# Seven products for eight in the second projection of a gated layer, on three of four blocks of tokens

## Chip, cores and metric

One core of one Trainium2 chip. The metric is the device time of one execution in microseconds; before and after are compared as medians of several executions. Engine names follow the profile: PE is TensorE's matmul stream and PEld its weight loads, DVE is VectorE, ACT is ScalarE, POOL is GpSimd, SP is the engine that issues most transfers.

## The reference

A transformer block in float32 on `x` of 2 x 1024 tokens and 256 features: self attention (16 heads of 64), cross attention to 154 context tokens, and a gated layer. All matmuls run in float32. What matters here is the last of the three:

```python
h = _layernorm(x, ln3_g, ln3_b)
p = h @ ff_w1 + ff_b1                 # 256 -> 2 x 1024
a, gate = (p[..., :D_FF], p[..., D_FF:])
h = a * jax.nn.gelu(gate, approximate=False) @ ff_w2 + ff_b2   # 1024 -> 256
return h + x
```

The second projection is the product of `a * gelu(gate)` (2048 tokens x 1024) with `ff_w2` (1024 x 256), added to the residual `x`.

## The kernel before

The whole kernel is recorded under a manual schedule: the order in which Python calls the helpers is the order in which each engine meets its instructions. Every engine has one queue and takes its instructions in that order. There are no due times or costs; the tile framework only adds the waits.

The attention stages fill the first 900 us. The gated layer then treats the 2048 tokens as NPR = 4 blocks ("pairs" in the code) of 512 tokens. A block is split into two token halves j of BT = 256 tokens. The 1024 inner features are NF = 8 chunks f of 128. A gate n = 8 * block + f (0 to 31) computes chunk f for the block's 512 tokens, by a seven-product scheme of its own (`product`, L1029): seven 128x128 by 128x256 products into three PSUM tiles `pa`, `pb`, `pc`. It is spread over two steps k of the main loop:

- Even k, `gate_first(n)`: product 1, then `gate_last(n - 1)` with product 4 of the gate before, products 6 and 5. So four products on PE.
- Odd k, `gate_second(n)`: products 2, 7, 3. So three products on PE.

The results go through ACT (a copy L1048, two GELUs L1066 and L1072) and DVE (L1052, L1054, L1068, L1071, L1080). POOL then multiplies value and gate into the buffers `ub[block][j][:, f, :]`: L1073 writes half j=1 (called from `gate_second`), L1082 writes half j=0 (called from `gate_last`, so one step later).

When gate f=7 of a block has been issued, the second projection of that block is queued in `sums`: 4 token tiles x 8 chunks = 32 slots, each one matmul (`sum_slot`, L1095) with 128 columns of `ub` as stationary operand and the 256 columns of `w2[:, f, :]` as moving operand. After the eighth chunk of a tile DVE adds the bank to the residual (L1105) and an output transfer is issued (L1106). Each step of the next block takes two slots from the queue, so 32 slots fill its 16 steps. The last block's slots run after the loop:

```python
            for _ in range(min(2, len(sums))):
                run(sum_slot)
            flush(stores)
            run_work(0 if k == 1 else 1 + k % 2, k % 2)
            if later and (k <= len(CG) + 2 or k > 2 * NF):
                later.pop(0)()
        gate_last(FU - 1)
        while sums:
            run(sum_slot)
            flush(stores)
```

POOL has other work in the same loop: the addition of the output bias to the residual (L324, one 128x256 addition in each step from k=17 to 31, popped from `later`) and the token sums of the gates' own scheme (`token_sums`, L1012 to L1015, four additions of 128x256 at k=8, 24 and 40).

PSUM: `sum_tile` and `mm_tile` have two banks each, `part_tile` four. `hold_gated` keeps both weight matrices of the layer in SBUF; `w2[:, f, d]` is chunk f of `ff_w2`.

Of the kernel before, what the change touches and what calls it, by code (L numbers as in the profile page):

```python
# [8 lines left out]
F32 = mybir.dt.float32  # L9
AF = mybir.ActivationFunctionType  # L10
ALU = mybir.AluOpType
AX = mybir.AxisListType

P = 128
# [4 lines left out]
def tile_transformer_block(ctx: ExitStack, tc: tile.TileContext, a: dict, out: bass.AP):  # L19
    nc = tc.nc  # L20
    x, cond = a["x"], a["ctx_768"]
    w = {k[len("L0_xattn_"):]: v for k, v in a.items() if k.startswith("L0_xattn_")}
# [9 lines left out]
    NT = S // P  # L32
    GT = 4
# [14 lines left out]
    QH = S // 2  # L48
    GH = QH // QG
    NK = HB // KB  # L50
    TG = HB // T
    NF = DF // P
    SH = GH // 2
    TF = 2
# [8 lines left out]
    pt_ = ctx.enter_context(tc.tile_pool(name="pt", bufs=2))  # L63
# [9 lines left out]
    def sum_tile(name):  # L73

        return ps_o.tile([P, HB], F32, tag="po", name=name)


    xt = {
        (b, g): const.tile([P, GT, D], F32, tag=f"x{b}{g}", name=f"x{b}{g}")
        for b in range(B) for g in range(NG)  # L80
    }
# [10 lines left out]
    names = ["ln1_g", "ln1_b", "ln2_g", "ln2_b", "ln3_g", "ln3_b", "ff_b1"]  # L92
# [5 lines left out]
    for n in names:  # L98
        k = n_of[n]
# [8 lines left out]
    for n in names[:2]:  # L108
        for r0 in range(0, P, HR):
            (nc.scalar if n == names[0] else nc.sync).dma_start(  # L110
                out=cols[r0:r0 + HR, row_of[n]:row_of[n] + NH],
                in_=w[n].rearrange("(r p) -> p r", p=HR),
# [54 lines left out]
    for n in names[2:]:  # L167
        own = rows[row_of[n] - n_cols:row_of[n] - n_cols + n_of[n], :]
        p = HR if n in twice else P
# [202 lines left out]
    def take_both(dst, pq, mul=None, t0=0, n=S // 2, shared=False):  # L372

        for r in range(2):
            k0, own = r * S // 2 + t0, pq[r][:, :n]
            if mul is not None:
                if shared and r:
                    nc.vector.tensor_scalar(
                        dst[:, k0:k0 + n], own, mul, 1.0, op0=ALU.mult, op1=ALU.mult)
                else:  # L380
                    nc.scalar.activation(dst[:, k0:k0 + n], own, AF.Copy, scale=mul)  # L381
                continue

            dk = dst.rearrange("p (h n j) -> p n h j", h=2, j=KB)[:, k0 // QG:(k0 + n) // QG]
            own = own.rearrange("p (n h j) -> p n h j", h=2, j=KB)
            if shared and r:
                nc.vector.tensor_copy(dk, own)
            else:
                nc.scalar.copy(dk, own)
# [172 lines left out]
    def run(piece):  # L562
        done = piece()
        if done is not None:
            (adds if getattr(done, "adds", False) else stores).append(done)

    def flush(queue):
        for fn in queue:
            fn()
        queue.clear()  # L570

    def run_work(n, n_side, bank=None, n_sum=0):

        while n > 0 and work:
            n -= work[0].banks
            run(work.pop(0))
        for _ in range(min(n_side, len(side))):  # L580
            needs_bank, needs, fn = side[0]
            if needs_bank and not bank and n <= 0 or not added.issuperset(needs):
                break
            if needs_bank and not bank:
                n -= 1
            spare["bank"] = bank or mm_tile
            run(fn)
            side.pop(0)
        for i in range(min(max(n, 0) + n_sum, len(outs))):
            spare["out"] = mm_tile if i < n else sum_tile  # L590
            run(outs.pop(0))
# [360 lines left out]
    NPR = B * 2  # L952
    BT = S // 4
    FU = NPR * NF
    wsum, wh, ub, psum, pools = {}, {}, {}, {}, {}

    def hold_gated():

        wf = pt_.tile([P, 2 * NK, QH // 2], F32, tag="pT", name="wf").rearrange("p a b -> p (a b)")
        n1, n2 = NC * 2 * DF, NF * D  # L960
        w1 = wf[:, :n1].rearrange("p (c h f) -> p c h f", c=NC, h=2)
        w2 = wf[:, n1:n1 + n2].rearrange("p (f d) -> p f d", f=NF)
        pTc["pairs"] = wf[:, n1 + n2:n1 + n2 + 2 * NM * 2 * NT * KB].rearrange(
            "p (a m j q) -> p a m j q", a=2, m=NM, j=2)

        def part1(c, h, f):
            f0 = h * DF + f
            nc.sync.dma_start(out=w1[:, c, h, f:f + HB], in_=w["ff_w1"][c * P:(c + 1) * P, f0:f0 + HB])

        def part2(f):  # L970
            nc.sync.dma_start(
                out=w2[:, f:f + 2, :],
                in_=w["ff_w2"][f * P:(f + 2) * P, :].rearrange("(f p) d -> p f d", p=P),
            )

        parts = [
            lambda c=c, h=h, f=f: part1(c, h, f)
            for c in range(NC) for h in range(2) for f in range(0, DF, HB)
        ]
        parts.extend(lambda f=f: part2(f) for f in range(0, NF, 2))  # L980
        return w1, w2, parts
# [39 lines left out]
    def product(n, i, into, first):  # L1021

        pair, f = divmod(n, NF)
        own = slice(f * P, (f + 1) * P)
        lhs = {
            1: w1[:, 0, 1, own], 2: w1[:, 1, 1, own], 3: wsum[4][:, own], 4: w1[:, 1, 0, own],
            5: wsum[1][:, own], 6: wsum[2][:, own], 7: w1[:, 0, 0, own],
        }[i]
        nc.tensor.matmul(  # L1029
            into[:, :BT], lhsT=lhs, rhs=wh[pair][i], start=first, stop=True,  # L1030
            skip_group_check=True)
# [24 lines left out]
    def biases(n):  # L1056
        c = row_of["ff_b1"] + n % NF
        return cols[:, c:c + 1], cols[:, c + NF:c + NF + 1]
# [16 lines left out]
    def gate_last(n):  # L1075

        pair, f = divmod(n, NF)
        pa, pb, pc, own = psum.pop(n)
        product(n, 4, pb, False)
        nc.vector.scalar_tensor_tensor(  # L1080
            own[:, 0, :], pb[:, :BT], biases(n)[0], own[:, 0, :], op0=ALU.add, op1=ALU.add)
        nc.gpsimd.tensor_tensor(ub[pair][0][:, f, :], own[:, 0, :], own[:, 3, :], ALU.mult)  # L1082
        if f == NF - 1:
            sums.extend((pair, i, e) for i in range(2 * TF) for e in range(NF))

    sums, summed = [], {}

    def sum_slot():

        pair, i, f = sums.pop(0)  # L1090
        if f == 0:
            summed[pair] = sum_tile(f"pf{pair}_{i}")
        own = summed[pair]
        j, e = divmod(i, TF)
        nc.tensor.matmul(  # L1095
            own[:, :D], lhsT=ub[pair][j][:, f, e * P:(e + 1) * P], rhs=w2[:, f, :],
            start=(f == 0), stop=(f == NF - 1),
        )
        if f < NF - 1:
            return None  # L1100
        b, t = divmod(pair * 2 * TF + i, NT)

        def store():
            xs = xt[b, t // GT][:, t % GT, :]
            nc.vector.tensor_tensor(xs, own[:, :D], xs, ALU.add)  # L1105
            (nc.scalar if pair == NPR - 1 and i % 2 else nc.sync).dma_start(  # L1106
                out=out[b, t * P:(t + 1) * P, :], in_=xs)

        return store


    with tc.manual_schedule():
# [11 lines left out]
        own = [ps_s.tile([P, 2, HB], F32, tag="s", name=f"first_{r}") for r in range(2)]  # L1124
# [7 lines left out]
        def take(what, i):  # L1132
            at = banks[what] if i < 2 else banks["k2"]
            take_both(qk["sa", 0, 0]["qk".index(what)], at, scale if what == "q" else None,
                      i * P, 2 * P, shared=True)
# [36 lines left out]
        for p in range(SA):  # L1172
# [18 lines left out]
            h, hg = divmod(p, SH)  # L1191
            ui, n = divmod(p, 2 * SH)
# [8 lines left out]
            if hg == LAG:  # L1201
                f = (ui - NPAIR // 2 - 1) * EC
# [10 lines left out]
        for c in range(CA):  # L1213
# [7 lines left out]
            if c == SH + 1:  # L1221

                w1, w2, parts = hold_gated()
# [3 lines left out]
            ui, n = divmod(c, len(CG))  # L1227
# [53 lines left out]
            elif n == 2:  # L1281
# [3 lines left out]
                elif ui == HP:  # L1285
                    wo["ca"] = const.tile([P, NPAIR, D], F32, tag="wo", name="ca_wo")
                    later[:0] = [lambda i=i: nc.sync.dma_start(
                        out=wo["ca"][:, i, :], in_=w["ca_wo"][i * P:(i + 1) * P, :])
# [20 lines left out]
        for k in range(2 * FU):  # L1309
            c = CA + k  # L1310
            if k == 0:
                run_work(0, 0, n_sum=2)
            flush(adds)
            (gate_second if k % 2 else gate_first)(k // 2)
            flush(stores)
            flush(lates)
            if k == 2 * len(CG) + 1:
                norm_beside("ff", B - 1)
            cross_drain(c)
            if k % 2:  # L1320
                cross_weigh(c - 1 if k == len(CG) + 2 else c)
            cross_regroup(c)
            if k == len(CG) + 2:
                out_pieces("ca", B - 1, NQ - 1, out_order("ca"))
            if k % (2 * NF) == NF and k < 2 * FU - 2 * NF:
                token_sums(k // (2 * NF) + 1)
            for _ in range(min(2, len(sums))):
                run(sum_slot)
            flush(stores)
            run_work(0 if k == 1 else 1 + k % 2, k % 2)  # L1330
            if later and (k <= len(CG) + 2 or k > 2 * NF):
                later.pop(0)()
        gate_last(FU - 1)
        while sums:
            run(sum_slot)
            flush(stores)


# [31 lines left out]
```

## Time and profile before

| | us |
|---|---|
| median of 3 runs | 1085.54 (1083.54 to 1085.69) |
| the profiled execution | 1084.96 |
| its span, first to last instruction | 1083.2 |
| PE busy in the span | 1067.0 |
| POOL busy | 727.1 |
| DVE busy | 878.7 |
| ACT busy | 643.5 |
| gated loop's gates 8 to 31 (950.60 to 1065.45) | 114.85 |
| second projection of the last block, from 1066.04 | 13.83 |

A line of the profile names the source line, engine, operation, the output and input tiles, and the shape; a PE matmul in float32 appears as two records. "Idle before" is how long the engine stood still ahead of an instruction, with the instruction that released it behind an arrow. PEclk is the clock granted to TensorE, as a share of full speed; it is 1.00 for this execution.

### The profile page before, as it was taken

What the parts mean: (1) busy time and instruction counts of PE and PEld (TensorE: products, weight loads), DVE (VectorE), ACT (ScalarE), POOL (GpSimd) and SP (SyncE); (2) the same over time, 40 slices, a digit from 0 to 9 for tenths busy, and PEclk for the clock granted to TensorE, in tenths of its full rate; (3) what the DMA queues carried; (4) which work ended last, traced back from release to release, by engine and by line L of the source; (5) the groups of instructions that cost most, each with busy time, mean ns of one, the idle gap of its engine ahead of it and who ended that gap; (6) DMA issues with size and microseconds to landing.
All of it is one profiled execution on the core that took longest, in us unless ns stands there. A gap on an engine that the chain in (4) does not pass through costs nothing.

```text
span 1083.2 us, 46388 instructions
## 1 busy us (share of the span) xinstructions
PE 1067.0 (99%) x19156; PEld 703.2 (65%) x19156; DVE 878.7 (81%) x1297; ACT 643.5 (59%) x2062; POOL 727.1 (67%) x1552
## 2 busy tenths in 40 slices
PE   8999999999999999999999999999999999999998
PEld 6556556556565565575665655566776677788887
DVE  5799999998989989999999889968877887654442
ACT  5766666777667657666776776656555554242321
POOL 2677777777777777677777777776756785475321
PEclk9999999999999999999999999999999999999999
DMA  3222122112111121111111101136765545000000
GB/s 91 68 70 52 39 48 53 43 43 50 32 43 34 30 50 38 34 43 34 33 42 25 43 14 38 29 79 150 191 157 125 119 107 118 1 10 15 11 14 30
DMA packets 104724, 60.81 MB, mean 56 GB/s; under 512 B 32378, under 2 KB 95298, under 8 KB 104514
## 3 DMA queue, kind: packets, MB, share of 16 engines
q1 hardware_dynamic: 103138, 57.07, 22.2%
q8 instruction: 151, 2.47, 1.0%
q10 hardware_dynamic: 1376, 0.79, 0.2%
q14 instruction: 59, 0.48, 0.1%
HBM read 27.91 MB, written 2.10 MB: 28 GB/s over the span
## 4 chain that ended last, share of the span: by engine, by line
PE 83%; DVE 4%; POOL 4%; DMA 3%; SPq 2%; ACT 2%; issue 1%; POOLq 0%; DVEq 0%; ACTq 0%
PE po L549 18%; PE s L497 17%; PE py_sa L471 5%; PE pf L1095 5%; PE py_ca L471 5%; PE pk_sa L366 4%; PE pv_sa L397 4%; PE poc L908 4%; PE pq_ca L366 4%; PE pq_sa L366 4%; PE pb L1029 4%; DMA st<-st 3%; PE sc L828 2%; PE pa L1029 2%; PE pc L1029 2%; SPq L518 2%
## 5 line engine op out<-in xcount | busy, mean ns | idle before, releaser
L619 POOL TENSOR_SCALAR p<-p,rd,ee 128x512 f32<-128x512 f32 x512 | 390.4, 768 | 90.8 <-DVE rd L609 87.7
L508 ACT ACTIVATE p<-s,st 128x512 f32<-128x512 f32 x512 | 345.0, 686 | 171.1 <-DVE st L681 163.7
L681 DVE TENSOR_REDUCE st<-s 128x2 f32<-128x1024 f32 x256 | 308.5, 1206 | 56.9 <-issue 19.0
L644 DVE STREAM_TRANSPOSE pT<-p 128x1024 f32<-128x1024 f32 x256 | 302.7, 1219 | 2.4 <-POOL p L619 2.1
L497 PE MATMUL s<-k_sa,q_sa 64*32 64x512 f32 x4096 | 252.8, 591 | 3.3 <-ACT p L508 2.5
L549 PE MATMUL po<-pT,v_sa 64*32 64x256 f32 x8192 | 237.1, 376 | 1.0 <-DVE pT L644 1.0
L549 PEld LDWEIGHTS po<-pT,v_sa 64*32 64x32 f32 x8192 | 172.9, 106 | 76.2 <-issue 31.2
L497 PEld LDWEIGHTS s<-k_sa,q_sa 64*32 64x32 f32 x4096 | 78.4, 106 | 104.6 <-issue 57.6
L845 ACT ACTIVATE p<-sc,neg 128x154 f32<-128x154 f32 x256 | 96.1, 403 | 83.0 <-DVE rden L853 79.3
L856 POOL TENSOR_SCALAR p<-p,rden 128x154 f32<-128x154 f32 x256 | 96.8, 398 | 56.7 <-DVE rden L853 56.5
L508 ACT ACTIVATION_READ_ACCUMULATOR p<-s,st 128x1 f32 x512 | 103.9, 203 | 0.0
L526 POOL TENSOR_TENSOR dd<-st 128x8 f32<-128x8 f32 x128 | 25.6, 200 | 74.9 <-DMA st<-st 73.0
L397 PEld LDWEIGHTS pv_sa<-sa_wv,hT_ln 64*128 64x128 f32 x1024 | 58.5, 188 | 14.2 <-issue 8.4
L397 PE MATMUL pv_sa<-sa_wv,hT_ln 64*128 64x128 f32 x1024 | 61.8, 275 | 0.0
L471 PE MATMUL py_ca<-ca_wo,o_ca 128*128 128x256 f32 x256 | 60.0, 382 | 0.5 <-DVE o_ca L922 0.5
L366 PE MATMUL pq_ca<-hT_ln,ca_wq 64*64 64x512 f32 (+1 forms) x544 | 60.1, 590 | 0.0
L471 PE MATMUL py_sa<-sa_wo,o_sa 128*128 128x256 f32 x256 | 59.7, 385 | 0.2 <-ACT v_sa L406 0.2
L471 PEld LDWEIGHTS py_sa<-sa_wo,o_sa 128*128 128x128 f32 x256 | 47.3, 190 | 18.2 <-issue 6.9
L834 DVE TENSOR_REDUCE neg<-sc 128x6 f32<-128x924 f32 (+1 forms) x48 | 47.9, 998 | 13.7 <-PE sc L828 13.3
L366 PE MATMUL pq_sa<-hT_ln,sa_wq 64*32 64x512 f32 (+1 forms) x976 | 56.6, 586 | 0.0
L366 PE MATMUL pk_sa<-hT_ln,sa_wk 64*32 64x512 f32 x960 | 56.2, 590 | 0.3 <-ACT q_sa L381 0.3
L845 ACT ACTIVATION_READ_ACCUMULATOR p<-sc,neg 128x1 f32 x256 | 56.1, 219 | 0.0
(121 smaller groups left out, 1418.9 us busy)
## 6 DMA issues: line engine op xcount, KB each, us to landing
wf<-pT_ca SPq DMA_DIRECT2D x128, 128.0 KB
st<-st SPq DMA_DIRECT2D x512, 1.0 KB
v_sa<-v_sa SPq DMA_DIRECT2D x32, 256.0 KB
sa_wq<-in_L_xattn_sa_wq_dram SPq DMA_DIRECT2D x32, 128.0 KB
sa_wk<-in_L_xattn_sa_wk_dram SPq DMA_DIRECT2D x32, 128.0 KB
sa_wv<-in_L_xattn_sa_wv_dram SPq DMA_DIRECT2D x32, 128.0 KB
ca_wq<-in_L_xattn_ca_wq_dram SPq DMA_DIRECT2D x32, 128.0 KB
wf<-in_L_xattn_ff_w_dram SPq DMA_DIRECT2D x12, 256.0 KB
```

The source lines that it names most:

```text
L366: nc.tensor.matmul(pq[r][f:f + m, at:at + n], lhsT=wt[own, c, f:f + m], rhs=h[own, c, t0:t0 + n], start=(c == 0), stop=(c == NH - 1), tile ...
L397: nc.tensor.matmul(pv[r][:, i * P:(i + 1) * P], lhsT=h[own, c, i * P:(i + 1) * P], rhs=wt[own, c, :], start=(c == 0), stop=(c == NH - 1), ...
L471: nc.tensor.matmul(py[:, e * D:(e + 1) * D], lhsT=o[:, i, (t + e) * P:(t + e + 1) * P], rhs=wo[kind][:, g * HP + i, :], start=(i == 0), st ...
L497: nc.tensor.matmul(sc[a4 * KB:(a4 + 1) * KB, j, :], lhsT=q[r, c:c + KB], rhs=k[r, h * HB:(h + 1) * HB], start=True, stop=True, tile_positi ...
L508: nc.scalar.activation(pr[:, j, :], sc[:, j, :], AF.Exp, bias=st[:, 0, 0, i, j:j + 1], accum_out=st[:, 0, 1, i, j:j + 1],)
L549: nc.tensor.matmul(po[a2][d:d + KB, :QH // 2], lhsT=v[r, t, e, d:d + KB], rhs=pT[r, d // DH * NK + n, :], start=(t == 0 and e == 0), stop= ...
L619: nc.gpsimd.tensor_scalar(pr[:, j, :], pr[:, j, :], own["rd"][:, c:c + 1], own["ee"][:, 0, c:c + 1], op0=ALU.mult, op1=ALU.mult,)
L644: nc.vector.transpose(halves[h][:, :, c:c + KB], slots[p]["p"][i].rearrange("p j (n k) -> p (j n) k", k=KB))
L681: nc.vector.tensor_reduce(st[:, 0, 0, i, :], sc[i], AX.X, ALU.max, negate=True)
L845: nc.scalar.activation(pr_[:, j, i, :T], sc[:, j, i * T:(i + 1) * T], AF.Exp, bias=neg[:, j, i:i + 1], accum_out=den[:, j, i:i + 1],)
L856: nc.gpsimd.tensor_scalar(pr_[:, j, i, :T], pr_[:, j, i, :T], rden[:, j, i:i + 1], 1.0, op0=ALU.mult, op1=ALU.mult,)
L1029: nc.tensor.matmul(into[:, :BT], lhsT=lhs, rhs=wh[pair][i], start=first, stop=True, skip_group_check=True)
```

## The change

For blocks 1, 2 and 3 (`FAST`) the second projection of each half j is computed as a 2x2 block product. The half's 256 tokens are two groups e of 128 tokens, its 1024 features are two groups of four chunks, and the 256 outputs are two groups of 128. Each of the resulting quarters of tokens A and weights B has four chunks. Seven products of quarters take the place of eight:

- Four sums of weight quarters T1 to T4 (`quick_weights`) are made once, on POOL, at steps k=22 to 25: four operations of 128x512.
- For each chunk c and half j, four sums of token quarters (`quick_tokens`) are made on POOL: S1, S2, S3 (written in place over A21) and S4, four operations of 128x128. They are queued in `combos` when gate f = 4 + c of the block has been issued, and popped four per step for k > 26; the rest follows after the loop.
- A unit g = 0 to 6 (`fast_sum`) is one product of quarters: four matmuls of 128 columns, accumulated over the four chunks. Units share banks: g=1 adds into the bank of g=0, g=3 and g=4 into that of g=2, g=6 into that of g=5. After each unit the bank is added to the residual: after g=0 by an ACT copy and a POOL addition of 128x384 (DVE in the last block), after the others by a DVE addition of 128x128.
- A step takes one unit (or two old slots). Block 0 keeps the 32 slots. Blocks 1 and 2 go half by half, j=0 then j=1; block 3 alternates j=1 and j=0 for each g.
- Output transfers of a half are issued after g=5 and g=6.

A sum made by POOL is read by PE: g=1 reads the gates' products of f=4 to 7, g=2 reads S2, g=3 reads S3, g=5 S1, g=6 S4. The new scratch tile `quick` takes the `pT` buffer that the cross attention leaves.

```diff
--- before.py
+++ after.py
@@ -1080,14 +1080,114 @@
         nc.vector.scalar_tensor_tensor(
             own[:, 0, :], pb[:, :BT], biases(n)[0], own[:, 0, :], op0=ALU.add, op1=ALU.add)
         nc.gpsimd.tensor_tensor(ub[pair][0][:, f, :], own[:, 0, :], own[:, 3, :], ALU.mult)
-        if f == NF - 1:
-            sums.extend((pair, i, e) for i in range(2 * TF) for e in range(NF))
-
-    sums, summed = [], {}
-
-    def sum_slot():
-
-        pair, i, f = sums.pop(0)
+        if pair in FAST and f >= NHF:
+            for j in (1, 0) if pair == NPR - 1 else (0, 1):
+                combos.extend(quick_tokens(pair, j, f - NHF))
+        if f == NF - 1 and pair in FAST:
+            order = [(j, g) for j in range(2) for g in range(7)]
+            if pair == NPR - 1:
+                order = [(j, g) for g in range(7) for j in (1, 0)]
+            sums.extend((lambda j=j, g=g: fast_sum(pair, j, g), 2) for j, g in order)
+        elif f == NF - 1:
+            sums.extend(
+                (lambda i=i, e=e: sum_slot(pair, i, e), 1) for i in range(2 * TF) for e in range(NF))
+
+    sums, summed, quick, combos = [], {}, {}, []
+    FAST = range(1, NPR)
+    NHF = NF // 2
+
+    def hold_quick():
+
+        own = pt_.tile([P, 2 * NK, QH // 2], F32, tag="pT", name="quick").rearrange("p a b -> p (a b)")
+        at = 0
+
+        def take(*dims):
+            nonlocal at
+            n = 1
+            for d in dims:
+                n *= d
+            view = own[:, at:at + n]
+            at += n
+            names = "abc"[:len(dims)]
+            return view.rearrange(
+                f"p ({' '.join(names)}) -> p {' '.join(names)}", **dict(zip(names, dims)))
+
+        for i in (1, 2, 3, 4):
+            quick["w", i] = take(NHF, P)
+        for i in range(3):
+            quick["u", i] = take(3, NHF, P)
+        for i in range(2):
+            quick["own", i] = take(P)
+
+    def quick_weights():
+
+        (b11, b12), (b21, b22) = (
+            [w2[:, h * NHF:(h + 1) * NHF, d * P:(d + 1) * P] for d in range(2)] for h in range(2))
+        t1, t2, t3, t4 = (quick["w", i] for i in (1, 2, 3, 4))
+        tt = nc.gpsimd.tensor_tensor
+        return [
+            lambda: tt(t1, b12, b11, ALU.subtract),
+            lambda: tt(t2, b22, t1, ALU.subtract),
+            lambda: tt(t3, b22, b12, ALU.subtract),
+            lambda: tt(t4, b21, t2, ALU.subtract),
+        ]
+
+    def quick_tokens(pair, j, c):
+
+        u, own = ub[pair][j], quick["u", (2 * pair + j) % 3]
+        (a11, a12), (a21, a22) = (
+            [u[:, h * NHF + c, e * P:(e + 1) * P] for h in range(2)] for e in range(2))
+        s1, s2, s4 = (own[:, i, c, :] for i in range(3))
+        tt = nc.gpsimd.tensor_tensor
+        return [
+            lambda: tt(s1, a21, a22, ALU.add),
+            lambda: tt(s2, s1, a11, ALU.subtract),
+            lambda: tt(a21, a11, a21, ALU.subtract),
+            lambda: tt(s4, a12, s2, ALU.subtract),
+        ]
+
+    def fast_sum(pair, j, g):
+
+        u, own = ub[pair][j], quick["u", (2 * pair + j) % 3]
+        (a11, a12), (a21, a22) = (
+            [u[:, h * NHF:(h + 1) * NHF, e * P:(e + 1) * P] for h in range(2)] for e in range(2))
+        lhs = (a11, a12, own[:, 1], a21, a22, own[:, 0], own[:, 2])[g]
+        rhs = (
+            w2[:, :NHF, :P], w2[:, NHF:, :P], quick["w", 2], quick["w", 3], quick["w", 4],
+            quick["w", 1], w2[:, NHF:, P:])[g]
+        if g in (0, 2, 5):
+            bank = sum_tile
+            if pair == NPR - 1:
+                bank = {0: sum_tile, 2: mm_tile, 5: part_tile}[g]
+            summed[j] = bank(f"pq{pair}_{j}_{g}")
+        into = summed[j][:, :P]
+        for c in range(NHF):
+            nc.tensor.matmul(
+                into, lhsT=lhs[:, c, :], rhs=rhs[:, c, :], start=(g in (0, 2, 5) and c == 0),
+                stop=(c == NHF - 1), skip_group_check=True)
+        b, t = divmod(pair * 2 * TF + 2 * j, NT)
+        xs = xt[b, t // GT][:, t % GT:t % GT + 2, :].rearrange("p t (h d) -> p (t h) d", d=P)
+
+        def store():
+            if g == 0:
+                nc.scalar.copy(quick["own", j], into)
+                (nc.vector if pair == NPR - 1 else nc.gpsimd).tensor_tensor(
+                    xs[:, 1:, :], xs[:, 1:, :],
+                    quick["own", j].unsqueeze(1).to_broadcast([P, 3, P]), ALU.add)
+                return
+            q = (None, 0, 1, 3, 2, 3, 1)[g]
+            nc.vector.tensor_tensor(xs[:, q, :], into, xs[:, q, :], ALU.add)
+            if g > 4:
+                e = 6 - g
+                queue = nc.scalar if pair == NPR - 1 and e else nc.sync
+                queue.dma_start(
+                    out=out[b, (t + e) * P:(t + e + 1) * P, :],
+                    in_=xt[b, (t + e) // GT][:, (t + e) % GT, :])
+
+        return store
+
+    def sum_slot(pair, i, f):
+
         if f == 0:
             summed[pair] = sum_tile(f"pf{pair}_{i}")
         own = summed[pair]
@@ -1324,15 +1424,29 @@
                 out_pieces("ca", B - 1, NQ - 1, out_order("ca"))
             if k % (2 * NF) == NF and k < 2 * FU - 2 * NF:
                 token_sums(k // (2 * NF) + 1)
-            for _ in range(min(2, len(sums))):
-                run(sum_slot)
+            n_left = 2
+            while n_left > 0 and sums:
+                fn, n = sums.pop(0)
+                n_left -= n
+                run(fn)
             flush(stores)
+            if k == 2 * NF + 2:
+                hold_quick()
+            if 2 * NF + 6 <= k < 2 * NF + 10:
+                if not combos:
+                    combos.extend(quick_weights())
+                combos.pop(0)()
+            elif k > 2 * NF + 10:
+                for _ in range(min(4, len(combos))):
+                    combos.pop(0)()
             run_work(0 if k == 1 else 1 + k % 2, k % 2)
             if later and (k <= len(CG) + 2 or k > 2 * NF):
                 later.pop(0)()
         gate_last(FU - 1)
+        while combos:
+            combos.pop(0)()
         while sums:
-            run(sum_slot)
+            run(sums.pop(0)[0])
             flush(stores)
```

## The prediction

> **What bounds the kernel now.** I read the page's busy shares and slices first, then a table of windows over the gated layer, then POOL's timeline where the change puts its additions, then the forms of weight loads and products.
>
> ```profile
> PE 1067.0 (99%) x19156; PEld 703.2 (65%) x19156; DVE 878.7 (81%) x1297; ACT 643.5 (59%) x2062; POOL 727.1 (67%) x1552
> ...
> PE   8999999999999999999999999999999999999998
> ```
>
> TensorE is busy to the end of the span, so removed products are removed time, if nothing else makes PE wait.
>
> ```profile
> 950.60:970.48 19.88, 19.88 (x99) 17.51 (x98) 9.27 (x23) 8.36 (x19) 13.10 (x21) 1.00 0.02 7
> 970.48:989.47 18.99, 18.99 (x89) 16.72 (x88) 9.32 (x22) 5.42 (x13) 13.86 (x20) 1.00 0.05 15
> 989.47:1027.46 37.99, 37.99 (x178) 33.44 (x177) 18.71 (x44) 10.84 (x25) 14.99 (x21) 1.00 0.04 14
> ```
>
> Columns: the window, its length, then busy PE, PEld, DVE, ACT, POOL, and PE's granted clock. The first two windows are block 1 (gates 8 to 11, then 12 to 15; one starts every 4.75 us), the third is block 2. PE never pauses. DVE and ACT have room. POOL is busy 27.0 of block 1's 38.9 us (the gates' products, the output bias, token sums) but only 15.0 of 38.0 in block 2.
>
> ```profile
> 970.86 0.73 POOL L1073 TENSOR_TENSOR u<-own 128x256 f32<-128x256 f32 x1 [1.97 <-ACT own L1072]
> 971.55 0.72 POOL L324 TENSOR_TENSOR x<-x,ff_b 128x256 f32<-128x256 f32 x1
> 972.23 0.73 POOL L1082 TENSOR_TENSOR u<-own 128x256 f32<-128x256 f32 x1
> 972.92 0.72 POOL L1012 TENSOR_TENSOR hs<-hT_ln 128x256 f32<-128x256 f32 x1
> 973.72 0.73 POOL L1013 TENSOR_TENSOR hs<-hT_ln,hs 128x256 f32<-128x256 f32 x1
> ```
>
> Start to start, a two-input 128x256 on POOL costs 0.685 us; one that needs the result just before it starts 0.80 after it, so such a dependence costs 0.11.
>
> ```profile
> L1095 PEld LDWEIGHTS pf<-wf,u 128*128 128x128 f32 x224 | 42.6, 190 | 5.8
> L1095 PE MATMUL pf<-wf,u 128*128 128x256 f32 x224 | 55.0, 379 | 0.0
> ```
>
> ```profile
> 14.74 1.86 PEld L366 LDWEIGHTS first_k<-hT_ln,sa_wk 64*128 64x128 f32 x32 [0.17 <-issue]
> ```
>
> ```profile
> 1066.04 13.83 PE pf L1095 x64
> ```
>
> These are forms of instructions (busy, mean ns), a timeline row of early weight loads, and the last row of the chain of waits. A product is two records. Sixty-four of 256 columns take 13.83 us: 0.216 each, with their 190 ns loads hidden.
>
> **TensorE's saving.** A block's second projection is now 32 products, 64 records, 13.83 us. After: two halves x 7 units x 4 products x 2 records = 112 records of 128 columns, each with a fresh 128-column load. No full-height row shows that. The nearest is the timeline row above: 64-row loads of 128 columns feeding 128 moving columns, two row groups side by side, 32 loads in 1.86 us. Per row group that is (1.86-0.19)/15 = 0.111; single records stand 0.112 apart. Lower bound 0.109 (transposes, L284, 128 columns); upper bound 0.19, the load's whole duration, if nothing overlapped. I take 0.112: the loads there are equally long (188 ns) and follow each other as fast. So 12.54 us, **-1.29 a block, -3.9 for three**. A unit is 8 x 0.112 = 0.90, against 0.86 for two slots before; a block has 14 units for 16 steps, so its last gate has none.
>
> [...]
>
> **What POOL gets.** In the built order, each of gates 4 to 7 of a block brings 8 additions of 128x128, in fours (`quick_tokens`). Price of one: two-input rows span 128x8 (next start after 0.17 to 0.28) to 128x256 (0.685); a straight line gives 0.42. From below, a one-input 128x154 stands 0.37 apart (L856), some 0.33 at 128; from above, 0.685. I take 0.42, since both ends have two inputs. A group of four has one immediate dependence: 4 x 0.42 + 0.11 = 1.79. The four weight sums, 128x512, come to 1.17 each on the same line; `fast_sum`'s 128x384 addition to 0.94.
>
> Per gate of two steps POOL then has in block 1: two products 1.37, two bias additions 1.37, two groups 3.58: 6.3 us, where PE passes in 4.75. The queue is in order, so the gate products that the sums read stand behind all this.
>
> **Block 1 to 2.** I follow POOL from 967.48 (L1082 of gate 10 in the trace). That product, a weight sum and a bias addition end at 970.02; gate 11's L1073 is ready at 970.86 as before. From there POOL never idles. L1073, weight sum, bias, L1082: 974.09. Token sums (2.85 in the trace): 976.94. Weight sum, bias, L1073 of 12, weight sum, bias, L1082, bias: 982.70. Then until L1082 of gate 15 is through: 6 products, 5 bias additions, 5 groups = 11 x 0.685 + 5 x 1.79 = 16.49, so 999.19. PE begins gate 16 at 989.47 (trace), then 1.73 (four products), unit g=0 0.90, three products 1.30: unit g=1 starts at 993.40, and its fourth product, wanting gate 15's result, at 994.07. With 0.1 for the signal (DVE to PE shows 0.06 at 945.06) PE **stops 5.2 us**. PE's later work is queued behind that matmul. Next, g=2 wants S2 of the last chunk: after 999.19 the 0.94, a group, L1073 of 16, then 0.42 + 0.53: 1003.55. PE arrives at 999.51 + 1.73 + 0.67 = 1001.91 and stops another **1.7**. Sum 6.9.
>
> **Block 2 to 3.** No bias additions. POOL takes up L1082 of gate 20 when ready, 1.63 after gate 21 starts. Until L1082 of gate 23 is through: 7 products 4.80, six groups 10.74, three more dependences 0.33, 1.0 of idle for gate 21's L1073: 18.5 after gate 21's start. PE wants it at 2 x 4.82 + 3.03 (gate 23 has no units) + 1.73 + 0.90 + 1.30 + 0.67 = 17.3. **Stop 1.3** with the signal.
>
> **The end.** Blocks' halves alternate, and 12 additions plus gate 31's last product remain on POOL. By the same queue, counted from gate 29's start: L1073 of 31 ends at 15.8, L1082 at 18.3, the two S2 at 19.3 and 21.1. PE finishes gate 31 at 13.45, including 0.35 because its last product follows L1068 without a unit between. It wants these at 15.9, 16.8, 19.3, and 20.3 as stops push it on: **0.35 + 1.6 + 0.05 + 0.9 = 2.9**.
>
> Hidden: fourteen ACT and DVE stores a block instead of four (128x256 takes 0.42 on DVE, 512 columns 0.69, so 128 about 0.29) have at least one gate step, or another unit of 0.90, before their bank is written again; without that cover each would cost about 0.5. At the end the last DVE addition is 0.13 shorter. Output transfers on SP wait behind nothing but each other, since SP has no other issues left in blocks 2 and 3; the last four leave within 3 us on two queues: 0 to 0.3, I take 0.
>
> **Sum:** -3.9 + 6.9 + 1.3 + 2.9 - 0.1 = **+7.1**. The profiled execution took 1084.96 us for a span of 1083.2, so 1092.1; the median of three is 0.6 higher. I say **1092.4 us**.
>
> The clock: the trace shows a start at half rate, the warm-up transposes 0.213 instead of 0.109 apart for 3.26 us, and no drop after stops of up to 1.08 us. A drop after the 5.2 us stop would lose 1.6 us, but PE waits 1.7 there for S2 anyway. I take 0, range 0 to 1.6.
>
> [...]
>
> **Rivals.** *POOL keeps up* (faster). One price decides: the 128x128 addition. At 0.33 (the one-input row) stops fall to about 4.3 and balance the saving; at 0.25 only the 0.35 is left: 1081.5. For it: POOL idles 23 us of block 2. Against: two-input rows cost 2.1 ns an element, and block 1's bias additions. 0.06 for clearly faster, 0.04 for a tie.
>
> *Loads bind* (slower still). At 0.19 a record a block takes 21.3 us, +7.5, and a slower PE leaves POOL 5.6 us of stops: -3.9 becomes +22.4, in all +28: 1113. Against: the 64-row rows. 0.05.
>
> *Forecast*, 0.85: the price from 0.36 (+2.5) to 0.50 (+14), 1087.5 to 1099, plus 1.6 of clock. Range with the tie's edge: 1086.5 to 1099.5. Measurement cannot tell less than about 0.2% (2.2 us) from no change. Faster 0.06, same 0.04, slower 0.90.
>
> **What would show it.** Right: PE idle before L1165 released by POOL, some 5 us near 994 and 2 near 1002, POOL without a gap from 971 to 1005, additions at L1143 to L1146 near 0.45 us long, and L1165 records 0.112 apart. Wrong: PE without gaps at 994, L1143 under 0.33 long, or L1165 0.19 apart.

## The result, and the profile after

The changed kernel takes 1092.19 us in the median (1091.17 to 1095.51), against 1084.54 us for the kernel before on the same chip (1082.49 to 1085.69): a ratio of 1.0080 over all executions, 95% interval 1.0063 to 1.0097 (the ratio of the two medians is 1.0071). It is slower, as forecast. The forecast was 1092.4 us.

The profiled execution of the changed kernel took 1095.51 us for a span of 1093.7 us, 3.3 us above the median. Its gate 16 starts at 991.35, 1.88 us later than in the trace of before, and PE's work ahead of that is the same and without a pause in the gates before. I therefore compare from gate 16 to the end of the span: 102.37 us here, 93.70 before, **+8.67 us**.

First the page's busy shares and slices:

```profile
PE 1070.7 (98%) x19300; PEld 708.1 (65%) x19300; DVE 884.7 (81%) x1323; ACT 645.5 (59%) x2068; POOL 779.9 (71%) x1656
...
PE   8999999999999999999999999999999999998998
```

POOL has 53 us more than before (779.9 for 727.1), and PE is below nine tenths in one more slice, the 37th (984 to 1012 us). The windows over the gated layer of the changed kernel show where (window, its length, busy PE, PEld, DVE, ACT, POOL, granted clock, DMA share, GB/s). The first line is gates 12 to 15, the second block 2, the third block 3's gates 24 to 30, then come four windows of 3.41 us:

```profile
972.36:991.35 18.99, 18.99 (x89) 16.72 (x88) 9.32 (x22) 5.42 (x13) 18.37 (x28) 1.00 0.05 15
991.35:1035.22 43.87, 38.69 (x225) 35.10 (x224) 20.35 (x52) 11.09 (x26) 35.41 (x66) 0.96 0.05 16
1035.22:1070.47 35.25, 34.14 (x212) 31.33 (x211) 18.72 (x49) 10.28 (x24) 24.23 (x46) 1.00 0.04 12
...
997.78:1001.20 3.42, 0.00 (x0) 0.00 (x0) 0.00 (x0) 0.00 (x0) 3.34 (x8) 1.00 0.00 0
1001.20:1004.61 3.41, 3.33 (x9) 2.79 (x10) 0.78 (x2) 0.37 (x1) 3.33 (x8) 0.50 0.00 0
...
1076.29:1079.70 3.41, 1.77 (x14) 1.39 (x13) 1.02 (x2) 0.08 (x1) 3.33 (x7) 1.00 0.00 0
1079.70:1083.12 3.42, 3.42 (x17) 3.42 (x18) 0.58 (x2) 0.00 (x0) 3.17 (x8) 0.50 0.00 0
```

While the sums are added in gates 12 to 15, POOL is busy 18.37 of 18.99 us (13.86 before) and PE still never pauses. The price comes after that: PE stands still for 5.2 us within block 2 and 1.1 us within block 3. The last lines show PE's clock at 0.50 for two stretches. PE's timeline shows each loss:

```profile
993.08 1.05 PE L1165 MATMUL pq<-wf,u 128*128 128x128 f32 x8
...
995.27 0.83 PE L1165 MATMUL pq<-wf,u 128*128 128x128 f32 x6
1001.28 0.80 PE L1165 MATMUL pq<-wf,u 128*128 128x128 f32 x2 [5.18 <-POOL u L1082]
1001.87 1.06 PE L1029 MATMUL pa<-hT_ln,wf 128*128 128x256 f32 x2
...
1004.96 1.18 PE L1165 MATMUL pq<-quick 128*128 128x128 f32 x8
...
1041.08 0.49 PE L1165 MATMUL pq<-wf,u 128*128 128x128 f32 x2 [1.11 <-POOL u L1082]
...
1079.54 0.67 PE L1165 MATMUL pq<-wf,u 128*128 128x128 f32 x2 [1.61 <-POOL u L1082]
1080.00 3.44 PE L1165 MATMUL pq<-quick 128*128 128x128 f32 x16
```

Three times the last product of a unit waits for POOL's L1082, the last gate's product, as named ahead. The row at 1001.87 is a gate product at half clock: two records in 0.85 us (to the next start) instead of 0.43. The row at 1080.00 has two units in 3.3 us instead of 1.8. POOL's timeline, with the price that the forecast had estimated, and the place where L1082 of gate 15 gets its turn:

```profile
985.47 0.46 POOL L1143 TENSOR_TENSOR quick<-u 128x128 f32<-128x128 f32 x1
986.00 0.46 POOL L1144 TENSOR_TENSOR quick<-quick,u 128x128 f32<-128x128 f32 x1
986.42 0.46 POOL L1145 TENSOR_TENSOR u<-u 128x128 f32<-128x128 f32 x1
986.83 0.46 POOL L1146 TENSOR_TENSOR quick<-u,quick 128x128 f32<-128x128 f32 x1
987.24 0.73 POOL L324 TENSOR_TENSOR x<-x,ff_b 128x256 f32<-128x256 f32 x1
...
1000.50 0.73 POOL L1082 TENSOR_TENSOR u<-own 128x256 f32<-128x256 f32 x1
```

The additions are 0.46 us long and 0.41 to 0.42 apart where none waits for the one before; a group of four takes 1.77 us from start to start (987.24 - 985.47). L1082 of gate 15 ends at 1001.23, 9.88 us after gate 16's start.

### The profile page after: what moved, and what is told of

It reads as the page before. It is cut to its first block, busy times and chain, and to the rows that moved or that the text cites. A ratio compares the mean times of both kernels' runs of the same rounds, so it can differ in the third digit from the quotient of the medians.

```text
span 1093.7 us, 46834 instructions
## 1 busy us (share of the span) xinstructions
PE 1070.7 (98%) x19300; PEld 708.1 (65%) x19300; DVE 884.7 (81%) x1323; ACT 645.5 (59%) x2068; POOL 779.9 (71%) x1656
## 4 chain that ended last, share of the span: by engine, by line
PE 81%; POOL 8%; DVE 3%; DMA 2%; SPq 2%; issue 1%; ACT 1%; POOLq 0%; DVEq 0%; ACTq 0%
PE po L549 18%; PE s L497 18%; PE py_sa L471 5%; PE py_ca L471 5%; PE pv_sa L397 5%; PE pk_sa L366 4%; PE pq_sa L366 4%; PE poc L908 4%; PE pq_ca L366 4%; PE pq L1165 3%; PE sc L828 3%; PE pb L1029 2%; SPq L518 2%; DMA st<-st 2%; PE pa L1029 2%; PE pc L1029 1%
```

## Experiments

Each run is set against executions of the kernel before on the same chip, so that kernel's median differs a little from run to run. Of each run I read how long a gate lasts (start to start), and how long it is from gate 31's start to the end of the last product ("end"). A gate with two units and no stop takes 4.81 us, one without units 3.02. Gates that are not listed can hold a loss too, which the text then names. The last column is the time from gate 16 to the span's end, against the kernel before.

| profiled run | gate 16 | 17 | 18 | 23 | 24 | end | from gate 16 on |
|---|---|---|---|---|---|---|---|
| before | 4.75 | 4.75 | 4.75 | 4.75 | 4.75 | 19.16 | 0 |
| changed | 10.52 | 6.29 | 4.81 | 3.02 | 6.18 | 20.33 | +8.67 |
| no sums | 4.81 | 4.81 | 4.81 | 3.02 | 4.81 | 16.54 | -3.67 |
| bias later | 4.81 | 6.51 | 4.81 | 3.02 | 8.66 | 19.63 | +6.39 |
| half on DVE | 7.37 | 6.48 | 4.81 | 3.70 | 5.18 | 18.09 | +3.34 |
| both of these | 4.81 | 5.74 | 4.81 | 4.09 | 5.18 | 18.61 | +1.13 |
| clock held | 10.29 | 6.55 | 4.81 | 3.02 | 6.18 | 19.65 | +8.01 |
| blocks 2 and 3 only | 4.75 | 4.75 | 4.75 | 4.75 | 4.81 | 19.63 | +0.71 |
| units a gate later | 3.08 | 7.18 | 6.86 | 4.81 | 3.08 | 19.63 | +2.20 |
| first half first | 4.81 | 4.81 | 4.81 | 3.02 | 4.81 | 19.70 | -0.51 |
| with shorter end | 4.81 | 4.81 | 4.81 | 3.02 | 4.81 | 18.09 | -2.14 |
| with S1, S2 first | 4.80 | 4.81 | 4.81 | 3.03 | 4.80 | 16.54 | -3.69 |

**No sums: what TensorE's saving is by itself.**

```diff
-            for j in (1, 0) if pair == NPR - 1 else (0, 1):
-                combos.extend(quick_tokens(pair, j, f - NHF))
...
-        lhs = (a11, a12, own[:, 1], a21, a22, own[:, 0], own[:, 2])[g]
+        lhs = (a11, a12, a22, a21, a22, a21, a12)[g]
```

The weights' sums are left out in the same way.

> The changed kernel without the sums of quarters: no weight sums, no token sums; the units multiply unsummed quarters in their place, with the same loads, shapes, banks and stores. Theory (POOL's late sums are the whole loss, TensorE's saving is real): PE never stops at a unit, 14 units of 0.89 us replace 13.83 us in each of three blocks, so about 3.6 to 4.1 us less than before: a ratio near 0.9965. Rival (units of 128 columns cost more than their records show, through banks shared by units or through the stores): no gain or a loss against before, with PE waiting for DVE or ACT at the units.

Measured: 1080.07 us (1078.96 to 1081.8) against 1084.4, ratio 0.9963 (0.9949 to 0.9977). No unit of products stops, and the only wait left is gate 31's own. So the seven products are worth what they were said to be; the whole loss is the price of the sums.

**Two ways to take load off POOL, alone and together.** The first moves eight of the bias additions past the end of block 1; the second gives VectorE the token sums of half j=1; the third does both.

```diff
-            if later and (k <= len(CG) + 2 or k > 2 * NF):
+            if later and (k <= len(CG) + 2 or 2 * NF < k < 3 * NF or k >= 4 * NF + 4):
```

```diff
-        tt = nc.gpsimd.tensor_tensor
+        tt = (nc.vector if j else nc.gpsimd).tensor_tensor
```

> The changed kernel with the last eight output bias additions moved from steps 24 to 31 to steps 36 to 43, the same additions on POOL at another place in its queue. Theory (the order in POOL's queue decides): 8 x 0.685 = 5.5 us leave the queue ahead of gate 15's product, so the stop at unit g=1 of block 1 falls from 5.2 to about 0, the wait for S2 stays at about 1.5, no half clock follows there; the rest is as in the changed kernel. About 5 us less than the changed kernel, so 2.5 to 3.5 above before, ratio near 1.003. Rival (the amount of work on POOL decides, wherever it stands): as the changed kernel, ratio near 1.007.

> The changed kernel with the token sums of half j=1 on DVE, half j=0 on POOL as now. Theory (POOL's backlog): two groups of 1.79 leave the queue ahead of gate 15's product, stop at g=1 of block 1 about 1.6 us, no wait for S2, no stop at block 2 to 3, and at the end 0.35: about 2 us below before, ratio near 0.998. Rival (moving 16 groups to DVE makes DVE the late engine, since its gate additions then stand behind sums that wait for POOL): PE stops released by DVE, no gain over the changed kernel.

> Both edits: half j=1's token sums on DVE and the eight bias additions at steps 36 to 43. Theory: no stop at a unit but 0.35 at the end, so the saving of TensorE stands alone, 3.6 to 4 us below before, ratio near 0.9965, equal to the kernel without sums within 0.5 us. Rival (DVE late): PE stops released by DVE at the gates, above the kernel without sums by 1 us or more.

Measured: bias later 1090.62 us, ratio 1.0056 (1.0042 to 1.0070); half on DVE 1086.77, ratio 1.0024 (1.0015 to 1.0034); both 1084.79, ratio 1.0006 (0.9997 to 1.0015), all against 1084.4. All three came out worse than the theory had it. The waits view (engine, tile and line <- releaser: us in total, times, longest) says why, together with the granted clock. Bias additions later:

```profile
PE pq L1165 <- POOL u L1082: 4.9, 2, 3.3
PE pq L1165 <- POOL quick L1144: 2.0, 2, 1.4
```

Gate 16's stop is gone as expected, but the additions now lie ahead of block 2's own sums in the queue, and gate 24 takes 8.66 instead of 6.18. The wait has changed its place. After it the clock stood at 0.50 from 1035.04 to 1038.45, which lengthens gate 25 as well, to 6.24.

With half on DVE the stop after gate 16 was 2.3 us where 1.6 had been worked out. Behind it the clock stood at 0.50 from 997.59 to 1001.00, and gate 17 took 6.48 us with no wait in it: here a half clock cost its 1.67 us in full. Waits for DVE (L1068, L1052) added 1.6.

With both changes it is VectorE that comes late:

```profile
PE pb L1029 <- DVE own L1068: 1.7, 1, 1.7
PE pb L1029 <- DVE own L1052: 0.8, 1, 0.8
```

DVE's timeline in the same run shows its price, first for an addition while POOL stood still (1061.11 to 1063.02), then for a group of four while POOL worked, and the gate's addition behind it:

```profile
1061.19 0.28 DVE L1145 TENSOR_TENSOR u<-u 128x128 f32<-128x128 f32 x1
...
1064.30 0.54 DVE L1143 TENSOR_TENSOR quick<-u 128x128 f32<-128x128 f32 x1
1064.87 0.43 DVE L1144 TENSOR_TENSOR quick<-quick,u 128x128 f32<-128x128 f32 x1
1065.22 0.54 DVE L1145 TENSOR_TENSOR u<-u 128x128 f32<-128x128 f32 x1
1065.68 0.81 DVE L1146 TENSOR_TENSOR quick<-u,quick 128x128 f32<-128x128 f32 x1
1066.41 0.47 DVE L1068 SCALAR_TENSOR_TENSOR own<-pb,cols,own 128x256 f32<-128x256 f32 x1
```

Over the run the four sums average 0.43 to 0.59 us on DVE against 0.28 undisturbed. Four undisturbed additions would be 1.1 us; this group takes 2.1 (1064.30 to 1066.41), and the gate's own additions (L1068, L1052), which PE waits for, stand behind it.

**The clock held up.** The changed kernel with transposes put ahead of the two matmuls that stop before a half clock.

```diff
+            if c == NHF - 1 and (j, g) == (0, 1):
+                for _ in range({1: 44, NPR - 1: 12}.get(pair, 0)):
+                    nc.tensor.transpose(summed[j][:, 2 * P:3 * P], ident, ident)
```

This run leaves the sums in the banks of these two units changed; the number and order of the kernel's own instructions are the same.

> The changed kernel with 44 transposes put ahead of the product that stops after gate 16 and 12 ahead of the one that stops at the end, so that TensorE stays active while it waits; nothing else is different. Theory (the prediction's: a half clock after the 5.2 us stop is hidden behind the wait for the second group of sums, so it costs nothing there, while the end's half clock costs about 1.7): the clock stays at 1.00 in both places, gate 17's first unit that uses a sum waits 1.5 to 1.9 us for GpSimd, the end is about 0.9 to 1.7 shorter; ratio 1.0065 to 1.0075. Rival (each half clock costs its 1.7 us in full): 3.4 us less than the changed kernel, ratio 1.005 or less.

(Its lines lie up to three lower.) Measured: 1091.7 us (1090.43 to 1093.66) against 1084.03, ratio 1.0069 (1.0055 to 1.0083), the clock 1.00 throughout. PE's timeline:

```profile
994.73 4.97 PE L1167 MATMUL pq<-ident 128*128 128x128 f32 x44
1000.11 0.49 PE L1168 MATMUL pq<-wf,u 128*128 128x128 f32 x2 [0.41 <-POOL u L1082]
...
1004.47 0.49 PE L1168 MATMUL pq<-quick 128*128 128x128 f32 x2 [1.48 <-POOL quick L1144]
```

After gate 16 the full clock wins nothing: PE arrives earlier and waits for S2 instead. Gates 16 and 17 take 16.84 us, against 16.81 with the half clock. At the end it wins 0.68 us (19.65 for 20.33). Of the rival's 3.4 us, 0.7 are there.

**Where along the queue the loss arises.** One kernel leaves block 1 with its eight products. The other is the changed kernel, but the units of blocks 1 and 2 begin one gate later.

```diff
-    FAST = range(1, NPR)
+    FAST = range(2, NPR)
```

```diff
-            n_left = 2
+            n_left = 0 if k >= 4 * NF and k % (2 * NF) < 2 else 2
```

> Block 1 keeps its eight products; only blocks 2 and 3 take seven. Theory (GpSimd too late after block 1's gates, because the bias additions share its queue): the 5.7 + 1.5 us of stops after gate 16 go, a saving of 1.33 us goes with them, and the stops after gate 24 (1.4) and at the end (4.2) stay: -2.7 + 5.6 = +2.9 us, ratio 1.0027, gates 16 and 17 4.75 to 4.8 us each. Rival (the loss is spread over all blocks, say by slower products beside GpSimd's sums): two thirds of the changed kernel's loss stay, +5 us, ratio 1.005.

> The changed kernel, all sums on GpSimd in its order, but the units of blocks 1 and 2 begin one gate later, so that it is the next block's first gate that has no units, not its own last one. Theory (a stop is GpSimd's finish minus the time at which TensorE wants it, and the gate without units ahead of it brings TensorE 1.8 us too early): TensorE wants gate 15's result 3.0 us later, the stops after gate 16 fall from 7.2 to about 2.3 and the one after gate 24 goes; the end stays at about 3.8; with -3.7 in all +2.4 us, ratio 1.0022, up to 1.7 us more if the 2.3 us stop halves the clock. Rival (GpSimd is short in all, the stops move on to the units that follow): 4 us or more of stops in gates 16 to 20, ratio 1.005 or more.

Measured: blocks 2 and 3 only 1085.17 us against 1084.03, ratio 1.0009 (1.0000 to 1.0018). Units a gate later 1086.31 against 1084.68, ratio 1.0019 (1.0010 to 1.0028).

The first was 2 us better than expected, because gate 24's stop was gone as well. In both traces L1082 of gate 23 is through at the same time after gate 23's start (8.83 us in the changed kernel, 8.93 here); but here gate 23 still has slots of block 1 beside it and lasts 4.75 us, where in the changed kernel it has no unit and lasts 3.02. So TensorE asks 1.7 us later and finds the result ready. The end lost no clock either (19.63, as with the clock held).

The second met its total by other parts than expected. Gate 24's stop is gone and gate 16's shrank from 5.5 to 2.3 us as worked out, but two more waits came after it (waits view, then DVE's timeline):

```profile
PE pq L1165 <- POOL u L1082: 2.6, 2, 2.1
PE pq L1165 <- POOL quick L1144: 1.1, 2, 0.6
PE pq L1165 <- DVE x L1179: 1.0, 1, 1.0
```

```profile
1004.25 0.29 DVE L1179 TENSOR_TENSOR x<-pq,x 128x128 f32<-128x128 f32 x1 [3.17 <-POOL x L1174]
```

A unit waits for a bank, the bank for DVE's store, and the store for POOL's L1174 on the same part of `x`: the theory had the first stop right and overlooked who stands behind POOL next. In gates 16 to 18, 4.5 us of stops remained where 2.3 were expected; that much the rival had named as its sign (4 us or more), though not with this total. It was made up at the end: block 2's last two units now lie in gate 31, ahead of the products that wait for POOL, and the stops there fell from 4.2 to 1.7.

**Less in POOL's queue ahead of a block's last product.** All sums stay on POOL, but in blocks 1 and 2 only those of the half that is multiplied first are made in the block's gates. The other half's are four additions of 128x512 in steps 2 to 5 of the next block. Four of the bias additions move from steps 28 to 31 to behind step 53.

```diff
-            for j in (1, 0) if pair == NPR - 1 else (0, 1):
+            for j in (1, 0) if pair == NPR - 1 else (0,):
                 combos.extend(quick_tokens(pair, j, f - NHF))
+            if f == NF - 1 and pair < NPR - 1:
+                bulk.extend(quick_tokens(pair, 1, slice(0, NHF)))
...
+            if bulk and 2 <= k % (2 * NF) < 6:
+                bulk.pop(0)()
...
-            if later and (k <= len(CG) + 2 or k > 2 * NF):
+            if later and (k <= len(CG) + 2 or 2 * NF < k < 3 * NF + 4 or k >= 6 * NF + 6):
```

> All sums stay on GpSimd, but in blocks 1 and 2 only those of the half that is multiplied first are made during the block's gates; those of the second half are four additions of 128x512 early in the next block, and the bias additions move away from both. Block 3 as in the changed kernel. Theory (what matters is how much GpSimd has queued ahead of the last gate's product at the block's end, not how much it does in all): the stops after gates 16 and 24 go, the end's 4.2 us stay against a saving of 4.0: ratio 1.000, between 0.998 and 1.002. Rival (GpSimd is short of time altogether, so the stops come back at the second half's first unit that uses a sum, or at the next chunk's gate products): 3 us or more of stops within gates 16 to 27, ratio 1.003 or more.

Measured: 1083.41 us (1081.35 to 1084.78) against 1084.03, ratio 0.9992 (0.9983 to 1.0000). POOL's busy time hardly changed (776.6 us for 779.9), and from gate 16 to gate 30 there is no stop at all, where the changed kernel has 8.6 us of stops. POOL's timeline, L1082 of gate 15 and the first of the larger additions:

```profile
991.34 0.72 POOL L1082 TENSOR_TENSOR u<-own 128x256 f32<-128x256 f32 x1
...
996.13 1.28 POOL L1145 TENSOR_TENSOR quick<-u 128x512 f32<-128x512 f32 x1
```

L1082 of gate 15 is through 3.83 us after gate 16's start (988.23), instead of 9.88. The larger additions, cheaper in all (1.28 us for one, against four of 0.46), come only behind it, so their price has no part in that. So POOL isn't short of time in these blocks. What counts is how much of its queue lies ahead of the product that PE wants next. The rest of the loss is the end; there one more kernel issues no group in step 63 and gives DVE the four sums of the last chunk for half j=1:

```diff
-        tt = nc.gpsimd.tensor_tensor
+        tt = (nc.vector if pair == NPR - 1 and (j, c) == (1, NHF - 1) else nc.gpsimd).tensor_tensor
...
-            elif k > 2 * NF + 10:
+            elif 2 * NF + 10 < k < 2 * FU - 1:
```

> As the run with the first half's sums first, and in block 3 the last gate's product goes ahead of the group of sums queued before it, while the four sums of that gate for the second half run on VectorE beside GpSimd's four for the first. Theory (the end's loss is GpSimd's queue ahead of gate 31's product plus the clock that the stop brings): the stop in the end falls from 1.6 to 0.5 us or less, the clock stays at 1.00, the end's loss falls from 4.2 to about 1, and the kernel is faster than both: -4.0 + 1.0 = -3.0 us, ratio 0.997. Rival (VectorE's sums, slow beside GpSimd's, hold back the last stores or the units that need them): end's loss 2.5 or more, ratio 0.9985 or more.

Measured: 1082.56 us (1080.87 to 1083.87), ratio 0.9985 (0.9976 to 0.9993): faster than the kernel before, but the end lost 2.0 us, not 1. L1082 of gate 31 is in time now; one wait is left, for S2 of the last chunk. POOL's timeline of this run (L1145 to L1148 are the four sums, two lines lower than in the changed kernel):

```profile
1066.12 0.51 POOL L1145 TENSOR_TENSOR quick<-u 128x128 f32<-128x128 f32 x1
1066.71 0.59 POOL L1146 TENSOR_TENSOR quick<-quick,u 128x128 f32<-128x128 f32 x1
1067.26 0.50 POOL L1147 TENSOR_TENSOR u<-u 128x128 f32<-128x128 f32 x1
1067.72 0.77 POOL L1148 TENSOR_TENSOR quick<-u,quick 128x128 f32<-128x128 f32 x1
1068.45 0.76 POOL L1145 TENSOR_TENSOR quick<-u 128x128 f32<-128x128 f32 x1
1069.29 0.45 POOL L1146 TENSOR_TENSOR quick<-quick,u 128x128 f32<-128x128 f32 x1
```

S2 of the last chunk (1069.29) stands behind S3 and S4 of the chunk before, which are wanted much later, and most of these additions are longer than 0.46 us while DVE makes its own. The last kernel changes two orders in block 3:

```diff
-                order = [(j, g) for g in range(7) for j in (1, 0)]
+                order = [(j, g) for g in (0, 1, 5, 2, 3, 4, 6) for j in (1, 0)]
...
-        while combos:
-            combos.pop(0)()
+        for i in (0, 1, 2, 3):
+            for fn in combos[i::4]:
+                fn()
```

The unit with S1 goes ahead of those with S2, and POOL makes S1 and S2 of the last groups first. (The output transfer of a tile moves along, to after its new last unit.)

> The run with the shorter queue at the end, with two orders changed in the last block: the unit that needs only S1 goes ahead of those that need S2, and GpSimd makes S1 and S2 of the last two chunks before their S3 and S4. Nothing is left out. Theory (the 1.4 us left at the end is S2 of the last chunk, standing behind S3 and S4 of the chunk before): that stop goes, the records from gate 31's start to the last are 16.1 to 16.5 us apart instead of 17.6, and the kernel loses nothing but gate 31's 0.4: from gate 16 on 3.5 to 3.7 us less than the kernel before, ratio 0.9965, the same as with no sums at all. Rival (VectorE and GpSimd slow each other at the end, or the stores come late): 1 us or more stays, ratio 0.9975 or more.

Measured: 1080.8 us (1080.73 to 1081.52) against 1084.68, ratio 0.9966 (0.9954 to 0.9978). It beats both kernels and loses nothing against the kernel without sums. PE's timeline has no wait for POOL in it (L1167 is L1165 of the changed kernel; each row is four units without a break):

```profile
1063.13 3.73 PE L1167 MATMUL pq<-wf,u 128*128 128x128 f32 x32
1066.70 3.74 PE L1167 MATMUL pq<-quick 128*128 128x128 f32 x32
1070.27 3.74 PE L1167 MATMUL pq<-quick,u 128*128 128x128 f32 x32
```

## Why the prediction was right

The sum, term by term, in the profiled execution of the changed kernel (the end is taken from the run with the clock held, and the clock's term is what the changed kernel's end took beyond that):

| term | said | measured |
|---|---|---|
| TensorE's saving and the shorter last addition | -4.0 | -4.1 |
| block 1 to 2, both stops | 6.9 | 7.2 |
| block 2 to 3 | 1.3 | 1.4 |
| the end | 2.9 | 3.5 |
| clock | 0 (0 to 1.6) | 0.7 |
| sum | 7.1 | 8.7 |

- **The saving.** The run without sums is 3.67 us shorter from gate 16 on, and holds 0.41 us of wait for L1068, which the prediction booked at the end: -4.1. A unit takes 0.89 us (993.08 to 993.97), so a record takes 0.112: the loads, 192 ns each in the median, are hidden, and the rival *loads bind* falls.
- **POOL's price.** 0.42 and 1.79 were estimated; it is 0.41 to 0.42 without a dependence, and 1.77 a group. This decided the rival *POOL keeps up*, which needed 0.33 for a tie and 0.25 to win. But POOL could have kept up at that price: the kernel with S1 and S2 first makes the same sums without a stop, with four additions given to DVE and 32 small ones made as eight larger. The prediction took the order of the queue as given, and as a forecast of this change that was right.
- **Block 1 to 2.** L1082 of gate 15 was to be through 9.72 us after gate 16's start (999.19 - 989.47); it was 9.88. The weight sums were put at 1.17 us each, but the straight line through 0.42 and 0.685 gives 1.22, and L1129 took that (970.05 to 971.27). The 5.2 and 1.7 us were 5.5 and 1.7 with the clock held.
- **The cover of the half clock.** "A drop after the 5.2 us stop would lose 1.6 us, but PE waits 1.7 there for S2 anyway": the half clock came (1001.20 to 1004.61), and cost nothing, since it took the place of the wait for S2, which the trace therefore does not show as an idle. The run with the clock held shows both. That the wait is what hid it shows in *half on DVE*, where none stood behind and 1.67 us were lost.
- **The mis-sized terms.** Both lie at the end. "0.35 + 1.6 + 0.05 + 0.9" measured 0.41 + 1.87 + 0.06 + 0.88 with the clock at 1.00, and 0.29 more for L1073 of gate 31, which the prediction had just in time. After each stop the second record is late by another 0.10 (included here), presumably because its load was held up too (PEld stands idle for 5.37, 1.30 and 1.80 us ahead of the three pairs of loads at 1001.28, 1041.08 and 1079.53). POOL finished L1073 0.27 and L1082 0.54 us later after gate 29's start than worked out (16.07 for 15.8, 18.84 for 18.3). Two of its rows there are long, and two of DVE's lie beside them:

```profile
1075.57 0.56 DVE L1174 TENSOR_TENSOR x<-x,quick 128x384 f32<-128x384 f32 x1 [0.76 <-ACT quick L1173]
1075.64 1.06 POOL L1073 TENSOR_TENSOR u<-own 128x256 f32<-128x256 f32 x1
1076.40 0.72 DVE L1174 TENSOR_TENSOR x<-x,quick 128x384 f32<-128x384 f32 x1 [0.28 <-ACT quick L1173]
1076.67 0.76 POOL L1143 TENSOR_TENSOR quick<-u 128x128 f32<-128x128 f32 x1
```

  Elsewhere L1073 takes 0.73 and L1143 0.46: together 0.63 us more (the run with two blocks has 1.05 and 0.77 at the same place). In the last block the change gives L1174 to DVE, and the prediction put no price on the two engines' additions meeting. No run moves L1174 away, so this cause is read from the rows alone. The clock, besides, was weighed only behind the 5.2 us stop. After the stop of 1.9 us at the end (start to start) it halved too, and made 16 records 1.6 us longer, of which the 0.9 us wait for S2 covered part: 0.7 remain.

That the medians differ by 7.65 us and these traces by 8.67 lies within the scatter of the changed kernel's four executions, 4.3 us. The forecast's 1092.4 thus hit the median more closely than its terms deserve: they were 1.6 us short in this execution.

## What to carry to other kernels

A sum of operands that saves products elsewhere is paid for in an in-order queue, and its price is not its busy time but what stands behind it: ask of every addition which waiting product it is queued ahead of. Before moving work to a second engine, try to change the order on the first: here the sums cost 12.3 us from gate 16 on in one order (+8.67 against -3.67 without them) and nothing in another, which gave DVE only four additions and made 32 small ones as eight larger. A stretch without units just ahead of a hand-over makes the consumer early, and so its wait longer: here gate 23 lasts 3.02 us without units, and 4.75 with slots beside it in the run with two blocks, where the stop of 1.1 us in gate 24 is gone.

## What the runs showed of the hardware that was not expected

**The half clock.** In the changed kernel both stretches at 0.50 behind a stop of PE, from 1001.20 and from 1079.70, last 3.41 us, and so do those in the run with the bias later (1035.04 to 1038.45) and with half on DVE (997.59 to 1001.00). The drop at 1079.70 followed a stop of 1.9 us. Stops of 1.9 us in the runs with two blocks and with the first half first, and of 2.3 us in the run with units a gate later, brought no drop in the profiled executions (granted clock 1.00). Yet two of the ten executions with two blocks show a mean clock of 0.998, so the same stop seems to cost clock in one execution and none in another. What decides it, these runs don't settle: in the 3.41 us ahead of the drop at 1079.70 PE was busy for 1.77, and after 3.41 us with 1.73 (994.37 to 997.78) the clock stayed at 1.00.

**VectorE beside GpSimd.** In the run with both changes, DVE's additions L1143 to L1146 (128x128) took 0.28 us while POOL stood still and 0.43 to 0.81 in the group from 1064.30 beside POOL's; one beside POOL's L1082 (1060.25) took 0.28 too. On POOL such an addition took up to 0.77 us beside DVE's (1067.72 in the run with the shorter end) instead of 0.46, and L1073 (128x256) 1.06 instead of 0.73 (1075.64 in the changed kernel). All these read SBUF alone. DVE's L1068, which also reads PSUM, kept its time: 0.48 us in the mean in the run with both changes and in the kernel before. Why the others lengthen, no run shows.
